# First image of a fused attention and cluster block: halves stored with 128 rows outermost, another order of its first stage, small weights loaded later

## The chip, the cores and the metric

The kernel runs on one core of a Trainium2 chip. The metric is the device time of one launch in microseconds (us); lower is better.

## The reference

The input x has 4 images of 256 channels and 64 x 64 pixels. Layer 0 is self-attention over the N = 4096 pixels of an image, with queries and keys of 32 channels:

```python
xf = x.reshape(B, C, N)
q = jnp.einsum('oc,bcn->bno', wq, xf) + bq
k = jnp.einsum('oc,bcn->bon', wk, xf) + bk[None, :, None]
attn = jax.nn.softmax(jnp.einsum('bnd,bdm->bnm', q, k), axis=-1)
v = jnp.einsum('oc,bcn->bon', wv, xf) + bv[None, :, None]
out = jnp.einsum('bcn,bmn->bcm', v, attn).reshape(B, Cc, H, W)
return gamma[0] * out + x
```

Layer 1 is a context-cluster block on the result: a group norm, features and values by 1x1 convolutions, an assignment of each pixel to one of four cluster centres per region and head, a projection added to x, then a second group norm with an MLP (1024 hidden channels, gelu), a scale and shift with relu, and a last 1x1 convolution with relu. All is float32. The change touches the start of layer 0 and the loading of weights.

## The kernel before, in words

An image is held in four SBUF tiles `xs[t]` of 128 partitions x 2 channel halves x 1024 pixels, each loaded by two DMAs of 512 KB (`load_x`). Blocks of NB = 512 pixels are the unit of queries and keys: NBLK = 8.

The order of the work is written out by hand (`tc.manual_schedule`): each engine, and SP as a queue of DMAs, runs its instructions in the order of the program. DMAs from SP and ACT share eight semaphores in turn, so a DMA can only be issued when the one eight places before it has landed. A DMA that waits holds back everything behind it on its engine, arithmetic included where the engine is ACT.

Attention of an image:

- **Projections and halves** (`halves_of`, L285 to L311). For four blocks at a time, PE makes queries or keys (`L295`): 4 row groups of 32 channels fill 128 partitions of a PSUM bank. ACT writes a rounded high half (`L304`), DVE the remainder as a low half (`L305`). Scores are then one product over 128 rows: queries stand as (high, high, low, low), keys as (high, low, high, low). That order is brought about through DRAM: four DMAs (`L311`) write the halves into a DRAM tile, and one DMA a block (`q_block` L355, `k_unit` L361) reads 128 rows of 512 back.
- `staged` (two projections into one PSUM tile with two banks) serves the first image twice ("first": keys and queries 0 to 3, "second": 4 to 7) and the queries of each later image, as `prepare`. `keys` makes the keys of later images, inside the cluster block of the image before.
- **Values** (`v_half`, `v_pair`): 16 pairs of value products (`L338`), each copied out of PSUM by ACT (`L346`). Two PSUM tiles are taken in turn.
- **Scores** (`score`, L375): unit u is one block of queries against one block of keys, 4 matmuls, copied out by ACT (L387, L388 or L397, L402), with running maxima on DVE (L392 or L399 to L404). `score(u)` first issues the read of keys u + 1. Two SBUF tiles hold keys.
- `fold`, `across`, `spread`: the maximum of a block over all keys, put on all partitions in PSUM (`mb`).
- **Weighting** (`weighting`): for 64 units, `exps` subtracts the maximum (DVE L480) and exponentiates (ACT L483), POOL sums (L485, L488), and PE accumulates values times weights (`weigh`, L493, 8 products of 512 columns a unit). Scores run ten units ahead. `prepare` of the next image is called at unit 61 of 64, after the fourth quarter of its `weigh`.

For the first image nothing comes before, so `alone` does it by itself: `staged("first")` with its half-writes issued by ACT, reads of keys 0 and queries 0 and 1, six value pairs, `staged("second")` with half-writes issued by SP, then eight scores with a value pair behind each, and two value pairs between the steps that make the maximum. For later images this lies inside the MLP of the image before.

At the very start the weights are loaded, in this order on SP: two loads of x tile 0, `wv_s`, `gbv`, x tiles 2 and 3, `pv_s`, `pc_s`, `h64`, `pool_w`, `mix` (two), `fvb`, `wproj_s` (two), `wpw_s`. ACT issues `wqk_s` (two), x tile 1 (two) and the query and key biases `bqk_s` (four). POOL turns two quarters of `wpw_s` (L147, L148) when they are there. `derived` (from L174), called at unit 1 of `weighting`, is the first reader of most of the small weights.

Of the kernel before, what the change touches and what calls it, by code (L numbers as in the profile page):

```python
# [46 lines left out]
def attention_then_cluster_block(  # L47
# [40 lines left out]
    def load_x(b, t, dma=nc.sync):  # L88
# [3 lines left out]
            dma.dma_start(out=xt[:, k, :], in_=xb[:, k, t * XT : (t + 1) * XT])  # L92
        return xt

    def loaded(name, ap, shape):
        t = const.tile(shape, F32, name=name)
        nc.sync.dma_start(out=t, in_=ap)
        return t

    xs0 = [load_x(0, 0)]
    wqk_s = const.tile([P, KC, 2, D], F32, name="wqk_s")
    for k in range(KC):
        nc.scalar.dma_start(out=wqk_s[:, k], in_=wqk[k * P : (k + 1) * P, :, :D])
    bqk_s = const.tile([P, 2], F32, name="bqk_s")
    xs0.append(load_x(0, 1, nc.scalar))
    for r in range(RG):
        nc.scalar.dma_start(
            out=bqk_s[r * D : (r + 1) * D, :], in_=pv[:D, PV["bq"] : PV["bq"] + 2]  # L110
        )
    wv_s = loaded("wv_s", wv.rearrange("(k p) m -> p k m", p=P), [P, KC, C])
    gbv = const.tile([P, KC], F32, name="gbv")
    nc.sync.dma_start(out=gbv, in_=bv.rearrange("(k p) -> p k", p=P))
    xs0 += [load_x(0, t) for t in range(2, N // XT)]
    pv_s = loaded("pv_s", pv, [P, NPV])
    pc_s = loaded("pc_s", pc.rearrange("(k p) n -> p k n", p=P), [P, KC, len(PC)])
# [1 line left out]

    pool_w = const.tile([P, 8, 32], F32, name="pool_w")  # L120
    nc.gpsimd.memset(pool_w, 0.0)
    nc.sync.dma_start(
        out=pool_w[:, :, :16], in_=consts[:, K_POOL : K_POOL + P].rearrange("p (j s) -> p j s", j=8)
    )

    own_w = {}
# [1 line left out]
    def load_mix(b):  # L128
        own_w["mix"] = swap.tile([P, KC, 2, 2 * ED + 32], F32, tag="mix", name=f"mix_{b}")
        for f in range(2):  # L130
            nc.sync.dma_start(
                out=own_w["mix"][:, :, f, 16 : 16 + 2 * ED],
                in_=wfv.rearrange("(k p) m -> p k m", p=P),
            )

    load_mix("first")
    fvb = const.tile([P, 2 * ED], F32, name="fvb")
    nc.sync.dma_start(out=fvb[:, ED:], in_=v_b.partition_broadcast(P))

    wproj_s = const.tile([ED + 1, C], F32, name="wproj_s")  # L140
    nc.sync.dma_start(out=wproj_s[:ED], in_=wproj)
    ipb = PC.index("proj_b")
    nc.sync.dma_start(out=wproj_s[ED:, :], in_=pc[:, ipb : ipb + 1].rearrange("c o -> o c"))

    wpw_s = loaded("wpw_s", wpw.rearrange("(k p) m -> p k m", p=P), [P, KC, C])
    pw_q = [wpw_s[:, k, h * P : (h + 1) * P] for k in range(KC) for h in range(2)]
    nc.gpsimd.tensor_tensor(pw_q[1], pw_q[1], pw_q[3], ALU.add)  # L147
    nc.gpsimd.tensor_scalar(pw_q[3], pw_q[3], -1.0, None, ALU.mult)  # L148

    ident = const.tile([P, P], F32, name="ident")  # L150
    make_identity(nc, ident)
# [80 lines left out]


    gab = const.tile([P, 2 * KC], F32, name="gab")
    probe = const.tile([P, 1], F32, name="probe")
    nc.gpsimd.memset(probe, 1.0)

    def table(f):

        nc.scalar.activation(probe, probe, f)  # L240
# [36 lines left out]
    def attention(b, xs):  # L277
# [4 lines left out]
        cells = small.tile([P, KC, NBLK, 4], F32, tag="cells", name=f"cells_{b}")  # L282
        qs, ks, slots, mxs, accs, tops, rdens, ts = {}, {}, {}, {}, {}, {}, {}, {}

        def halves_of(which, i, parts, ps, dma=nc.sync):  # L285

            col = 1 if which == "k" else 0  # L290
            if which not in own:
                own[which] = dram.tile([NBLK, 4, D, NB], F32, tag=which, name=f"{which}_{b}")
            for k in range(KC):
                for r in range(RG):
                    nc.tensor.matmul(  # L295
                        ps[r * D : (r + 1) * D],
                        wqk_s[:, k, col],
                        block(xs, k, 4 * i + r),
                        start=(k == 0),
                        stop=(k == KC - 1),  # L300
                    )
            bias = bqk_s[:, col : col + 1]
            hi, lo = parts
            nc.scalar.activation(hi, ps, AF.Identity, bias=bias)  # L304
            nc.vector.scalar_tensor_tensor(  # L305
                lo, ps, bias, hi.bitcast(F32), ALU.add, ALU.subtract
            )
            rows = own[which][4 * i : 4 * i + 4]
            for c in range(4):
                part = hi if c in ((0, 2) if which == "k" else (0, 1)) else lo  # L310
                dma.dma_start(out=rows[:, c], in_=part.bitcast(F32))  # L311

        def staged(name, which, dma=nc.sync):


            st = spool.tile([P, 4, NB], F32R, tag="s", name=f"st_{b}_{name}")
            ps = ps_s.tile([P, 2, NB], F32, tag="s", name=f"pr_{b}_{name}")
            for j, (w, i) in enumerate(which):
                halves_of(w, i, (st[:, 2 * j], st[:, 2 * j + 1]), ps[:, j], dma)

        def keys(i):

            ps = ps_m.tile([P, NB], F32, tag="m", name=f"kp_{b}_{i}")
            parts = [
                big.tile([P, NB], F32R, tag="k", bufs=2, name=f"hl{j}_{b}_{i}") for j in range(2)
            ]
            halves_of("k", i, parts, ps)

        vps = {}

# [17 lines left out]
        def v_pair(i):  # L348
            v_half(2 * i)
            v_half(2 * i + 1)  # L350

        def q_block(nb):

            qs[nb] = work.tile([P, NB], F32R, tag="q", name=f"q_{b}_{nb}")
            nc.sync.dma_start(out=qs[nb].bitcast(F32), in_=own["q"][nb].rearrange("c d n -> (c d) n"))  # L355

        def k_unit(u):

            g = u % GRP
            ks[u] = big.tile([P, NB], F32R, tag="k", bufs=2, name=f"k_{b}_{u}")  # L360
            nc.sync.dma_start(out=ks[u].bitcast(F32), in_=own["k"][g].rearrange("c d n -> (c d) n"))  # L361

        def score(u, hooks=None, later=None):

# [181 lines left out]

        def alone():

            staged("first", (("k", 0), ("q", 0)), nc.scalar)
            k_unit(0)  # L550
            q_block(0)
            q_block(1)
            for i in range(6):
                v_pair(i)
            for u in range(GRP):
                if u == 0:
                    staged("second", (("k", 1), ("q", 1)))
                hooks, maxima = [], []
                score(u, hooks, maxima)
                for f in hooks + maxima:  # L560
                    f()
                v_pair(u + 6)
            fold(0)
            half["dg"] = across(0)
            v_pair(GRP + 6)
            spread(0, half["dg"])
            v_pair(GRP + 7)
            exps(0)
            score(GRP)

# [25 lines left out]
        def weighting(ahead, fill, early, prepare):  # L596
# [3 lines left out]
            for u in range(units):  # L600
                nb, g = divmod(u, GRP)
                more = nb + 1 < NBLK
                if g == 0:
                    av = [
                        ps_a.tile([P, NB], F32, tag=f"a{c}", name=f"av{c}_{b}_{nb}")
                        for c in range(KC)
                    ]
                if g + 1 < GRP:
                    exps(u + 1)
                else:  # L610
                    gather(nb)
# [24 lines left out]
                weigh(u, av, 2)  # L636
                if g == GRP - 2 and more:
                    known(nb + 1, mb)
                due(u, 3)
                if g == GRP - 3 and more:  # L640
                    mb = highest(nb + 1)
                weigh(u, av, 3)
                if u == 1:
                    early()
                if u in biased:

                    t, c = biased[u]
                    nc.scalar.activation(
                        xs[t][:, c], xs[t][:, c], AF.Identity, bias=gbv[:, c : c + 1]
                    )  # L650
                if u == units - 3:
                    prepare()
                if g == 3 and nb + 2 < NBLK:
                    q_block(nb + 2)
                if g == GRP - 1 and more:
                    clear(nb, av)
# [1023 lines left out]
```

## Time and profile before

| | us |
|---|---|
| median of 3 runs (3314.1 to 3314.88) | 3314.72 |
| the profiled execution | 3316.3 |
| its span | 3314.5 |
| ACT busy in the span | 1679.6 |
| DVE busy | 2231.4 |
| POOL busy | 1929.9 |
| PE's weight loads (PEld, beside PE) | 1930.3 |

The span is that of the instructions in the profiled execution; the execution's own time is 1.8 us more. The mean granted TensorE clock is 0.991 of full speed. PE is TensorE's matmuls, ACT ScalarE, DVE VectorE, POOL GpSimd, SP SyncE; ACTq and SPq are DMA issues by those engines. A line of the timeline has start and length in us, engine, kernel line, operation, output and inputs, count, and in brackets how long the engine had stood idle and what released it.

From the timeline of the first 100 us, in order: the first projection starts at 5.21, the first high half at 13.59 (after the biases and a table load of 1.28), the first half-writes are issued at 14.31, the value products go on at 32.90, the second projections at 42.00, the first score at 47.37, the second at 69.78, the eighth at 87.88, and the first weighting product at 99.85. Each from the third to the eighth score, with its value pair, takes 2.65.

### The profile page before, as it was taken

What the parts mean: (1) busy time and instruction counts of PE and PEld (TensorE: products, weight loads), DVE (VectorE), ACT (ScalarE), POOL (GpSimd) and SP (SyncE); (2) the same over time, 40 slices, a digit from 0 to 9 for tenths busy, and PEclk for the clock granted to TensorE, in tenths of its full rate; (3) what the DMA queues carried; (4) which work ended last, traced back from release to release, by engine and by line L of the source; (5) the groups of instructions that cost most, each with busy time, mean ns of one, the idle gap of its engine ahead of it and who ended that gap; (6) DMA issues with size and microseconds to landing.
All of it is one profiled execution on the core that took longest, in us unless ns stands there. A gap on an engine that the chain in (4) does not pass through costs nothing.

```text
span 3314.5 us, 33083 instructions
## 1 busy us (share of the span) xinstructions
PE 3220.7 (97%) x11114; PEld 1930.3 (58%) x11114; DVE 2231.4 (67%) x3570; ACT 1679.6 (51%) x2253; POOL 1929.9 (58%) x1358
## 2 busy tenths in 40 slices
PE   4999999999999999999999999999999999999999
PEld 3544444778744444478864444447884444446786
DVE  1776775577777677466767777746776777765665
ACT  2655553445565555344556555535455555544444
POOL 0467567266457667636646667663654676673663
PEclk7999999999999999999999999999999999999999
DMA  4111112100111111210011111121011111110000
GB/s 143 51 51 42 48 48 91 45 26 29 36 58 48 48 45 42 102 40 26 29 42 51 48 39 54 41 105 36 20 39 54 41 53 48 39 52 1 13 20 26
DMA packets 87002, 154.78 MB, mean 47 GB/s; under 512 B 12496, under 2 KB 21296, under 8 KB 86832
## 3 DMA queue, kind: packets, MB, share of 16 engines
q1 hardware_dynamic: 84752, 149.45, 13.9%
q10 hardware_dynamic: 2080, 3.21, 0.3%
q8 instruction: 88, 1.44, 0.2%
q14 instruction: 82, 0.67, 0.1%
HBM read 118.96 MB, written 33.67 MB: 46 GB/s over the span
## 4 chain that ended last, share of the span: by engine, by line
PE 90%; DVE 5%; DMA 1%; ACT 1%; issue 1%; POOL 1%; SPq 0%; ACTq 0%; DVEq 0%; POOLq 0%
PE av L493 52%; PE mo L1309 9%; PE sc L375 7%; PE hq L1392 5%; PE hp L1392 3%; PE hr L1392 3%; PE fv L888 3%; PE vp L338 2%; PE mo L1293 1%; PE hq_pw L1392 1%; DVE st L993 1%; PE pw L1248 1%; PE hr_pw L1392 1%; PE hp_pw L1392 1%; DMA k<-k 1%
## 5 line engine op out<-in xcount | busy, mean ns | idle before, releaser
L493 PE MATMUL av<-s,v 128*128 128x512 f32 x4096 | 1796.3, 592 | 0.7 <-ACT s L483 0.7
L488 POOL TENSOR_TENSOR acc<-acc,s 128x1024 f32<-128x1024 f32 x448 | 1060.2, 2367 | 502.3 <-ACT s L483 481.8
L493 PEld LDWEIGHTS av<-s,v 128*128 128x128 f32 x4096 | 775.8, 190 | 896.1 <-issue 866.7
L483 ACT ACTIVATE s<-s 128x1024 f32<-128x1024 f32 x512 | 541.0, 1058 | 569.2 <-DVE s L480 549.0
L480 DVE TENSOR_TENSOR s<-s,mb 128x1024 f32<-128x1024 f32 x512 | 595.7, 1205 | 16.2 <-ACT mb L464 14.9
L401 DVE TENSOR_TENSOR top<-sc,top 128x1024 f32<-128x1024 f32 x196 | 239.1, 1220 | 291.1 <-PE sc L375 291.1
L1347 ACT ACTIVATE hs<-hs,pv_s 128x256 f32<-128x256 f32 x496 | 232.4, 502 | 343.1 <-DVE hs L1383 343.1
L375 PE MATMUL sc<-q,k 128*128 128x512 f32 x1024 | 371.1, 484 | 22.1 <-DMA k<-k 19.4
L1309 PE MATMUL mo<-hs,w 128*128 128x256 f32 x1512 | 385.2, 381 | 0.0
L1309 PEld LDWEIGHTS mo<-hs,w 128*128 128x128 f32 x1512 | 283.8, 190 | 46.3 <-ACT hs L1347 6.8
L404 DVE TENSOR_TENSOR top<-sc,top 128x1024 f32<-128x1024 f32 x196 | 240.0, 1225 | 81.5 <-ACT s L397 69.1
L375 PEld LDWEIGHTS sc<-q,k 128*128 128x128 f32 x1024 | 191.0, 189 | 160.9 <-issue 121.1
L397 ACT COPY s<-sc 128x1024 f32<-128x1024 f32 x224 | 224.6, 1003 | 116.1 <-PE sc L375 83.5
L402 ACT COPY s<-sc 128x1024 f32<-128x1024 f32 x224 | 227.6, 1016 | 109.8 <-DVE top L401 73.7
L1383 DVE TENSOR_TENSOR hs<-hq,hs 128x256 f32<-128x256 f32 x496 | 198.3, 420 | 79.6 <-PE hq L1392 69.6
L485 POOL TENSOR_TENSOR acc<-s 128x1024 f32<-128x1024 f32 x32 | 75.9, 2371 | 288.1 <-ACT s L483 288.0
L1316 POOL TENSOR_TENSOR hs<-hs 128x256 f32<-128x256 f32 x108 | 82.2, 761 | 184.3 <-ACT hs L1400 86.2
L338 PE MATMUL vp<-wv_s,x 128*128 128x256 f32 x512 | 133.1, 407 | 14.2 <-ACT v L346 14.2
L1383 DVE TENSOR_TENSOR hs<-hp,hs 128x256 f32<-128x256 f32 x124 | 52.1, 420 | 115.0 <-ACT hs L1400 115.0
L1392 PE MATMUL hr<-xn,w 128*128 128x256 f32 x496 | 127.8, 380 | 0.5 <-DVE hs L1383 0.5
L338 PEld LDWEIGHTS vp<-wv_s,x 128*128 128x128 f32 x512 | 99.5, 202 | 41.0 <-ACT v L346 16.4
L1392 PEld LDWEIGHTS hr<-xn,w 128*128 128x128 f32 x496 | 94.4, 191 | 18.0 <-issue 3.3
(271 smaller groups left out, 3501.5 us busy)
## 6 DMA issues: line engine op xcount, KB each, us to landing
k<-k SPq DMA_DIRECT2D x256, 256.0 KB
out<-xn SPq DMA_DIRECT2D x62, 256.0 KB
x<-in_x SPq DMA_DIRECT2D x30, 512.0 KB
q<-q SPq DMA_DIRECT2D x32, 256.0 KB
w<-in_w SPq DMA_DIRECT2D x8, 1024.0 KB
mr<-row_mx SPq DMA_DIRECT2D x28, 256.0 KB
rden<-row_rd SPq DMA_DIRECT2D x28, 256.0 KB
q<-st_queries SPq DMA_DIRECT2D x24, 256.0 KB
```

Of the source, the lines that this page charges most:

```text
L338: nc.tensor.matmul(vps[0][:, i % 2, :], xs[i * P // XT][:, k, o : o + P], wv_s[:, k, :], start=(k == 0), stop=(k == KC - 1),)
L375: nc.tensor.matmul(halves[r // 2][:, r % 2, :], k_s[:, r * P : (r + 1) * P], q_s, start=True, stop=True,)
L401: nc.vector.tensor_tensor(top, halves[1], top, ALU.max)
L404: nc.vector.tensor_tensor(top, halves[0], top, ALU.max)
L480: nc.vector.tensor_tensor(sh, sh, mxs[nb].unsqueeze(1).to_broadcast([P, 2, NB]), ALU.subtract)
L483: nc.scalar.activation(sh, sh, AF.Exp)
L488: nc.gpsimd.tensor_tensor(acc, acc, s[:, 2 * h : 2 * h + 2], ALU.add)
L493: nc.tensor.matmul(av[c], own["v"][:, RG * g + quarter, c * P : (c + 1) * P], slots[u][:, quarter, :], start=(g == 0 and quarter == 0), st ...
L1309: return nc.tensor.matmul(bank[:, half * HB : (half + 1) * HB], a[:, j], t, start=start, stop=stop)
L1347: nc.scalar.activation(src, src, AF.Gelu_apprx_tanh, bias=pvc("b1", P, j + 4 * (i > 1)))
L1383: nc.vector.tensor_tensor(dst, ps, term, ALU.add)
L1392: nc.tensor.matmul(out, w, x, start=True, stop=True)
```

## The change

1. **Layout in DRAM.** The DRAM tiles for halves were (block, 4 parts, 32 channels, 512 pixels); a half-write went to 4 blocks x 32 channels x 512. They become (4 blocks together, 128 rows, 4 parts, 512 pixels), so a half-write goes to 128 rows x 512. A block is read as its 32 rows x 4 parts; each still is one contiguous 256 KB. It holds for all images.
2. **Projections first.** `halves_of` is split: `projected` (PE alone) and `halves_of` (ACT, DVE and DMAs). `staged` makes both projections before any half.
3. **First image** (`alone`). The ACT table is loaded ahead; three value pairs come before `staged("first")`, whose half-writes are issued by SP; five pairs follow, then scores with pairs 8 to 15 behind them, so that none is left between the steps of the maximum.
4. **Loads.** `wv_s` is loaded ahead of x tile 1 in program order and stands third on SP as before; the four biases are issued by POOL. `gbv`, `pv_s`, `pc_s`, `h64`, `pool_w`, `wpw_s`, and `mix`, `fvb`, `wproj_s` are issued by SP after score 3 and its value pair (`load_rest`), with POOL's two operations on `wpw_s` behind them. On SP this is 11 DMAs after the read of keys 4 and before that of keys 5.
5. **Queries of later images**: `prepare` at unit 62 instead of 61.

The work of PE, ACT, DVE and POOL is the same in kind and number, but for the ACT table's one probe instruction.

```diff
+    probe = const.tile([P, 1], F32, name="probe")
+    nc.gpsimd.memset(probe, 1.0)
+    behind = []
     def loaded(name, ap, shape):
         t = const.tile(shape, F32, name=name)
-        nc.sync.dma_start(out=t, in_=ap)
+        behind.append(lambda: nc.sync.dma_start(out=t, in_=ap))
         return t
...
+    wv_s = const.tile([P, KC, C], F32, name="wv_s")
+    nc.sync.dma_start(out=wv_s, in_=wv.rearrange("(k p) m -> p k m", p=P))
     bqk_s = const.tile([P, 2], F32, name="bqk_s")
     xs0.append(load_x(0, 1, nc.scalar))
     for r in range(RG):
-        nc.scalar.dma_start(
+        nc.gpsimd.dma_start(
             out=bqk_s[r * D : (r + 1) * D, :], in_=pv[:D, PV["bq"] : PV["bq"] + 2]
         )
-    wv_s = loaded("wv_s", wv.rearrange("(k p) m -> p k m", p=P), [P, KC, C])
-    gbv = const.tile([P, KC], F32, name="gbv")
-    nc.sync.dma_start(out=gbv, in_=bv.rearrange("(k p) -> p k", p=P))
+    gbv = loaded("gbv", bv.rearrange("(k p) -> p k", p=P), [P, KC])
...
+    def load_rest():
+        load_mix("first")
+        nc.sync.dma_start(out=fvb[:, ED:], in_=v_b.partition_broadcast(P))
+        nc.sync.dma_start(out=wproj_s[:ED], in_=wproj)
+        nc.sync.dma_start(out=wproj_s[ED:, :], in_=pc[:, ipb : ipb + 1].rearrange("c o -> o c"))
+        for f in behind:
+            f()
+        nc.gpsimd.tensor_tensor(pw_q[1], pw_q[1], pw_q[3], ALU.add)
+        nc.gpsimd.tensor_scalar(pw_q[3], pw_q[3], -1.0, None, ALU.mult)
...
-        def halves_of(which, i, parts, ps, dma=nc.sync):
+        def projected(which, i, ps):
             col = 1 if which == "k" else 0
-            if which not in own:
-                own[which] = dram.tile([NBLK, 4, D, NB], F32, tag=which, name=f"{which}_{b}")
             for k in range(KC):
                 for r in range(RG):
                     nc.tensor.matmul(
...
+        def halves_of(which, i, hi, lo, ps, dma=nc.sync):
+            col = 1 if which == "k" else 0
+            if which not in own:
+                own[which] = dram.tile([NBLK // RG, P, 4, NB], F32, tag=which, name=f"{which}_{b}")
             bias = bqk_s[:, col : col + 1]
-            hi, lo = parts
             nc.scalar.activation(hi, ps, AF.Identity, bias=bias)
...
-            rows = own[which][4 * i : 4 * i + 4]
+            rows = own[which][i]
             for c in range(4):
                 part = hi if c in ((0, 2) if which == "k" else (0, 1)) else lo
                 dma.dma_start(out=rows[:, c], in_=part.bitcast(F32))
+        def stacked(which, nb):
+            i, r = divmod(nb, RG)
+            return own[which][i, r * D : (r + 1) * D].rearrange("d c n -> (d c) n")
...
             for j, (w, i) in enumerate(which):
-                halves_of(w, i, (st[:, 2 * j], st[:, 2 * j + 1]), ps[:, j], dma)
+                projected(w, i, ps[:, j])
+            for j, (w, i) in enumerate(which):
+                halves_of(w, i, st[:, 2 * j], st[:, 2 * j + 1], ps[:, j], dma)
...
         def alone():
-            staged("first", (("k", 0), ("q", 0)), nc.scalar)
+            table(AF.Identity)
+            for i in range(3):
+                v_pair(i)
+            staged("first", (("k", 0), ("q", 0)))
             k_unit(0)
             q_block(0)
             q_block(1)
-            for i in range(6):
+            for i in range(3, 8):
                 v_pair(i)
             for u in range(GRP):
                 if u == 0:
...
-                v_pair(u + 6)
+                v_pair(u + GRP)
+                if u == 3:
+                    load_rest()
             fold(0)
             half["dg"] = across(0)
-            v_pair(GRP + 6)
             spread(0, half["dg"])
-            v_pair(GRP + 7)
             exps(0)
             score(GRP)
...
-                if u == units - 3:
+                if u == units - 2:
                     prepare()
```

More of the change, by code (lines that the diff above doesn't have):

```diff
@@ L121, in attention_then_cluster_block @@
     nc.gpsimd.memset(pool_w, 0.0)
-    nc.sync.dma_start(
-        out=pool_w[:, :, :16], in_=consts[:, K_POOL : K_POOL + P].rearrange("p (j s) -> p j s", j=8)
+    behind.append(
+        lambda: nc.sync.dma_start(
+            out=pool_w[:, :, :16],
+            in_=consts[:, K_POOL : K_POOL + P].rearrange("p (j s) -> p j s", j=8),
+        )
     )
@@ L134, in load_mix @@
             )
-    load_mix("first")
     fvb = const.tile([P, 2 * ED], F32, name="fvb")
-    nc.sync.dma_start(out=fvb[:, ED:], in_=v_b.partition_broadcast(P))
     wproj_s = const.tile([ED + 1, C], F32, name="wproj_s")
-    nc.sync.dma_start(out=wproj_s[:ED], in_=wproj)
     ipb = PC.index("proj_b")
-    nc.sync.dma_start(out=wproj_s[ED:, :], in_=pc[:, ipb : ipb + 1].rearrange("c o -> o c"))
+    def load_rest():
[7 more added lines that the diff above has]
+        nc.gpsimd.tensor_scalar(pw_q[3], pw_q[3], -1.0, None, ALU.mult)
     wpw_s = loaded("wpw_s", wpw.rearrange("(k p) m -> p k m", p=P), [P, KC, C])
     pw_q = [wpw_s[:, k, h * P : (h + 1) * P] for k in range(KC) for h in range(2)]
-    nc.gpsimd.tensor_tensor(pw_q[1], pw_q[1], pw_q[3], ALU.add)
-    nc.gpsimd.tensor_scalar(pw_q[3], pw_q[3], -1.0, None, ALU.mult)
     ident = const.tile([P, P], F32, name="ident")
@@ L234, in attention_then_cluster_block @@
     gab = const.tile([P, 2 * KC], F32, name="gab")
-    probe = const.tile([P, 1], F32, name="probe")
-    nc.gpsimd.memset(probe, 1.0)
     def table(f):
@@ L326, in keys @@
             ]
-            halves_of("k", i, parts, ps)
+            projected("k", i, ps)
+            halves_of("k", i, *parts, ps)
         vps = {}
@@ L354, in q_block @@
             qs[nb] = work.tile([P, NB], F32R, tag="q", name=f"q_{b}_{nb}")
-            nc.sync.dma_start(out=qs[nb].bitcast(F32), in_=own["q"][nb].rearrange("c d n -> (c d) n"))
+            nc.sync.dma_start(out=qs[nb].bitcast(F32), in_=stacked("q", nb))
         def k_unit(u):
@@ L360, in k_unit @@
             ks[u] = big.tile([P, NB], F32R, tag="k", bufs=2, name=f"k_{b}_{u}")
-            nc.sync.dma_start(out=ks[u].bitcast(F32), in_=own["k"][g].rearrange("c d n -> (c d) n"))
+            nc.sync.dma_start(out=ks[u].bitcast(F32), in_=stacked("k", g))
         def score(u, hooks=None, later=None):
```

## The prediction

> **What bounds the kernel now.** I read part 1 of the page first, then busy time by stretch, then the timeline of the first 125 us with the chain of waits, and last every stretch in which PE stands still.
>
> ```profile
> PE 3220.7 (97%) x11114; PEld 1930.3 (58%) x11114; DVE 2231.4 (67%) x3570; ACT 1679.6 (51%) x2253; POOL 1929.9 (58%) x1358
> ```
>
> PE works 97% of the span: only its 94 us of idle time (3314.5 - 3220.7) and time at a reduced clock can be won. The stretches (PE busy, PEld, DVE, ACT, POOL, then PEclk, DMA share, GB/s) show where they lie:
>
> ```profile
> 5.20:20.70 15.50, 11.12 (x48) 4.07 (x48) 1.50 (x2) 2.66 (x3) 0.00 (x0) 1.00 0.80 250
> 20.70:32.90 12.20, 0.00 (x1) 0.00 (x1) 0.00 (x0) 0.64 (x2) 0.00 (x0) 0.61 0.52 162
> ...
> 51.50:69.80 18.30, 0.02 (x1) 0.06 (x1) 0.64 (x2) 0.59 (x1) 0.00 (x0) 0.57 0.33 122
> 69.80:90.60 20.80, 20.80 (x84) 17.41 (x84) 15.79 (x26) 16.35 (x20) 0.00 (x0) 0.89 0.28 77
> 90.60:99.90 9.30, 6.30 (x29) 4.40 (x27) 6.12 (x8) 2.90 (x6) 0.00 (x0) 1.00 0.08 28
> ...
> 585.00:605.00 20.00, 20.00 (x71) 11.30 (x72) 7.30 (x9) 6.03 (x8) 8.73 (x6) 1.00 0.26 100
> ```
>
> About 45 us of PE's idle time lie before 100 us, most of it in two holes of 12.2 and 18.3 us. In both, few of the DMA engines work. The timeline names the holders, and the chain says the same of the second hole:
>
> ```profile
> 32.26 1.07 ACT L346 COPY v<-vp 128x512 f32<-128x512 f32 x2 [13.38 <-DMA q<-st_first]
> 32.90 9.17 PE L338 MATMUL vp<-wv_s,x 128*128 128x256 f32 x32 [12.21 <-ACT v L346]
> ...
> 69.78 2.04 PE L375 MATMUL sc<-q,k 128*128 128x512 f32 x4 [18.28 <-DMA k<-k]
> 71.62 3.33 PE L338 MATMUL vp<-wv_s,x 128*128 128x256 f32 x8
> ...
> 583.00 1.92 PE L295 MATMUL pr_queries<-x,wqk_s 128*32 128x512 f32 x16 [1.65 <-DVE st_queries L305]
> ```
>
> ```profile
> 52.16 3.56 SPq L311
> 55.77 2.52 SPq L311
> 58.33 11.31 DMA k<-k
> ```
>
> First hole: ACT's queue also issues the eight writes of the first halves, each behind a DMA still in flight, so the copies of v that free PSUM come at 32.26. Second hole: SP issues eight more half-writes, then the read of keys 1, which lands at 69.6. At 583.00 PE waits 1.65 us for DVE between two projections; this recurs at 1394.67 and 2207.06 (images 1 to 3 being prepared).
>
> **What the skill says.** (1) "DMA: Bandwidth & Descriptors", section on why a DMA increments its semaphore by 16: a DMA runs on the largest k up to 16 that divides the slowest dimension of both patterns. The old DRAM side is 4x32x512, so k = 4; the new is 128x512, so 16. The trace agrees on the old: in 585 to 605, when only query half-writes run, the share is 0.26 at 100 GB/s, a quarter of the engines. (2) "TensorE: Matmul & The Clock Gate", Part 1: the array runs at half clock until some 3.4 us of activity. Agrees: PEclk 0.57 in the second hole; the two groups after it took 2.04 and 3.33 us where the same groups at 80 us take 1.28 and 1.89, a loss of 2.2. (3) The DMA page, "SWDGE vs HWDGE vs iDMA" and "Latency": DMAs from GpSimd have software-made descriptors, about 1 us to the first byte, some 2 us fixed. No DMA here is issued from POOL, so nothing shows it.
>
> **The change, part by part.** *Half-writes.* 262144 bytes at 100 GB/s are 2.6 us, eight 21 us. Sixteen engines at the same rate each (100/0.26 = 385 GB/s) give 0.68 us, eight 5.4 us: an estimate. The completion records support it: the output store, same rows on 16 engines, ends 2.1 us after issue. Reads are contiguous as before (2.6 us to landing).
>
> *The new order of the first image*, step by step:
> - PE starts with three value products and needs wv, complete at 8.9 in the records of before, behind the same two x loads: 8.9 against 5.2. This is a loss of 3.7 us.
> - Three products at 1.73 (a period of 80.80 to 83.45 is 2.65, of which scores take 0.92) are 5.2, plus 2.2 for the half clock: 16.3. Copies of v (0.58) keep up, ACT no longer issues half-writes and its table is loaded early (1.28 us, under the wait for x).
> - Keys and queries are projected together, 2 x 1.8: 19.9. The halves then follow as ACT 0.69, DVE 0.75, ACT 0.69, DVE 0.75 = 2.9, beside PE's next five products (8.7): 28.6; second projections 3.6: 32.2.
> - SP issues the first half-writes from 20.7 to 24.0; eight at 0.68 from 1.2 after the first issue end about 27.8. q block 0 is read after that, 2.8 us: 30.7. Score 0 wants it at 32.2: 1.5 us of cover. Its second PSUM half waits for DVE until 35.2 (0.93 and 1.59 us of such gaps were there before, 2.7 now). Product 8 ends at 37.5.
> - SP issues the second half-writes from 33.0; data 34.2 to 39.6; the read of keys 1 is behind all eight in SP's order and lands at about 40.4. PE waits 2.9. **Score 1: 40.4 instead of 69.8.**
> - Scores 1 to 7 are six periods of 2.65 (ACT 2.64, DVE 2.5 a period stay below): 15.9.
>
> *Small weights behind score 3.* The function issues 11 DMAs on SP after the read of keys 4 and before keys 5; their issues in the timeline sum to 5.2 us. Keys 4 goes out when score 2 is done, 44.1; so keys 5 at 49.6 rather than when score 3 is done (46.7), landing 52.3 to 53 behind wpw's 256 KB; score 5 wants it at 51.0. I charge 1.5; the lower end is 0, the upper 4.5, if a lane wait holds SP. The two POOL operations on wpw go ahead of POOL's first sum: free. What reads these weights (L174 at 113.9) comes 60 us after their issue.
>
> *Clock.* The PE gaps of 2.7 and 2.9 us may drop the clock: a 1.85 us gap did at 1484, one of 2.29 at 93 did not. One window of 3.4 us costs 1.7, two 3.4; I charge 1.5. Score 7 then starts at 40.4 + 15.9 + 1.5 + 1.5 = 59.3, against 87.88: 28.6 earlier.
>
> *Tail.* Products 14 and 15 leave it. They hid nothing there, as the DVE chain (maxima, fold, reduce, subtract) sets its length, and the copy of product 15 delayed the exponentials: 0.7 gained. PE is emptier there and may go cold: 0.5 charged (0 to 2), the rest under the 1.68 us gap at 124.16, which DVE and ACT set. Net 28.8.
>
> *Bias bqk from POOL.* Four DMAs, bounded by 0 and 4 x 3 = 12 us (page's figures, an estimate) after 0.9: at worst 13, needed at 19.9, so free with 7 us of cover. ident and the memsets queued behind on POOL are first needed at the fold.
>
> *Queries of later images.* Both projections before the halves remove 3 x 1.65 = 5.0. Moving them one unit later puts the last exponentials (DVE L480 at 586.38, behind the halves) ahead; after it PE has a unit of 16 products (6.9 us) as cover, and the sum on POOL (to 594.9) ends earlier. The half-writes on SP come 6 us later but end sooner; their reader is 60 us away. The faster key writes free SP only: no PE gap there waits on them.
>
> Sum: 28.8 + 5.0 = **33.8**. From the profiled span 3314.5 that is 3280.7 (its execution took 3316.3, 1.8 around the span); from the median 3314.72, 3280.9. I say **3281**.
>
> **Rivals.**
> - *Everything aligns:* no clock drop, keys 5 in time, and ACT allowed to split keys before the query projection ends: 1.5 + 1.5 + 1.8 = 4.8 more, 3276. For: the halves are separate banks. Against: before, the second projection waited for DVE on the first half, so the whole tile is tracked.
> - *More waits in its place:* keys 5 late by 4.5 (+3), two cold windows at score 1 and in the tail (+3.4), wv late by 1.5: gain 26, 3289. For: all sit on PE's path without cover.
> - *The query gaps aren't worth their length*, as the end of an image is a chain over DVE and POOL: 3286. Against: PE runs without a gap from 583 to 650.
> - *The layout doesn't spread the DMAs:* eight first writes end at 43, eight second at 64, score 1 at 65.5: gain 4.3 + 0.7 + 5.0 = 10, 3305. Against: the output store's 128 rows.
> - *Slower: bqk is late.* ACT waits in order for it before the first half; behind it stand the copies of v, so PE stops within two products. Each us after 19.9 costs one; from 19.9 + 33.8 = 54 us on the kernel is slower, at 60 it gives 3321. Only an unseen start-up cost of POOL's DMA path could do that.
>
> **How the numbers follow.** Forecast 52%, aligned 14%, more waits 15%, query gaps 11%, no spread 3% (2 of them inside the bound), late bqk 5% (1 inside the bound). Less than 0.2% (6.6 us) can't be told from no change here: faster 52 + 14 + 15 + 11 + 1 = 0.93; same 0.03; slower 0.04. Range 3273 to 3292: from the aligned case less some us of an earlier wv (0 to 3) to the upper ends of clock and keys 5. It leaves out no spread, late bqk and part of the tails.
>
> **What would show it.** Half-write stretches at a DMA share well over 0.26; no ACT copy of v waiting for a DMA; no hole of 12 or 18 us; score 1 near 40, keys 5 late by a few us behind the small weights, the first weighting product near 71; no 1.65 us gap in pr_queries. I am wrong if L316 waits for bqk, if keys 1 lands after 45, or if PE's gap reappears at the end of an image.

## The result and the profile after

The changed kernel takes 3290.24 us (median of 4 runs, 3289.91 to 3290.54) where the kernel before, on the same chip, takes 3314.8 (3314.1 to 3315.07): a ratio of 0.9926 [0.9909, 0.9943], 24.6 us less. Run again beside an experiment it gave 3288.4 against 3315.04, 0.9919 [0.9905, 0.9932]. The forecast was 3281 with a range of 3273 to 3292: the direction and most of the size hold, 9 us of the expected 33.8 did not come. Of these, 7.2 are in the profiled executions too (spans 3314.5 and 3287.9, so 26.6); the rest is that the profiled execution of before was 1.5 us above its median and that of after 0.3 below.

PE's line on the first part of the page of after:

```profile
PE 3220.5 (98%) x11114; PEld 1933.6 (59%) x11114; DVE 2232.6 (68%) x3570; ACT 1680.7 (51%) x2254; POOL 1933.1 (59%) x1362
```

PE is as busy as before (3220.7), in a span 26.6 us shorter. So it is idle time that went, 94 us down to 67. Busy time by stretch shows from where (after; start and end, length, then busy PE, PEld, DVE, ACT, POOL, then PEclk, which is the granted share of the TensorE clock, DMA share, GB/s):

```profile
8.79:20.60 11.81, 11.81 (x57) 7.45 (x57) 0.00 (x0) 1.76 (x3) 0.00 (x0) 1.00 0.47 191
20.60:32.96 12.36, 12.36 (x73) 8.39 (x73) 1.50 (x2) 4.20 (x7) 0.00 (x0) 1.00 0.67 234
32.96:42.32 9.36, 3.12 (x15) 2.11 (x13) 2.80 (x4) 3.88 (x5) 0.00 (x0) 0.97 0.82 278
42.32:57.89 15.57, 12.17 (x48) 9.99 (x49) 9.99 (x16) 9.77 (x12) 0.91 (x2) 0.91 0.54 128
57.89:64.77 6.88, 6.88 (x24) 5.60 (x25) 3.23 (x6) 4.19 (x5) 0.09 (x1) 0.75 0.20 53
64.77:76.56 11.79, 7.21 (x24) 4.33 (x22) 8.70 (x12) 4.22 (x6) 0.00 (x0) 0.86 0.11 38
...
571.00:574.00 3.00, 3.00 (x8) 1.10 (x6) 0.29 (x1) 0.00 (x0) 0.00 (x0) 1.00 1.06 380
```

The two holes of 12.2 and 18.3 us are gone: from 8.79 to 32.96 PE has no idle time at all, and the first half-writes lie under its work (second row). The last row, where only query half-writes run, has a DMA share of 1.06 at 380 GB/s; the like stretch before had 0.26 at 100. The third and fourth rows hold what is left of the two holes, 6.2 and 3.4 us, and the timeline of after names it:

```profile
8.79 8.21 PE L358 MATMUL vp<-wv_s,x 128*128 128x256 f32 x24 [8.79 <-DMA wv_s<-in_wv]
...
20.66 0.69 ACT L316 ACTIVATE st_first<-pr_first,bqk_s 128x512 fp32r<-128x512 f32 x1 [3.04 <-PE pr_first L299]
21.38 2.10 SPq L323 DMA_DIRECT2D k<-st_first  x4
...
36.16 0.70 PE L395 MATMUL sc<-q,k 128*128 128x512 f32 x2 [2.50 <-DVE st_second L317]
...
38.34 9.48 SPq L381 DMA_DIRECT2D k<-k  x4
...
42.32 2.05 PE L395 MATMUL sc<-q,k 128*128 128x512 f32 x4 [3.73 <-DMA k<-k]
...
47.88 0.94 SPq L139 DMA_DIRECT2D mix_first<-in_wfv  x2
...
51.50 1.27 PE L395 MATMUL sc<-q,k 128*128 128x512 f32 x4
...
52.13 0.47 SPq L103 DMA_DIRECT2D h<-in_consts  x1
...
53.42 0.37 SPq L128 DMA_DIRECT2D pool_w<-in_consts  x1
...
54.52 21.70 SPq L381 DMA_DIRECT2D k<-k  x6
...
57.89 1.27 PE L395 MATMUL sc<-q,k 128*128 128x512 f32 x4 [3.40 <-DMA k<-k]
58.96 3.51 PE L358 MATMUL vp<-wv_s,x 128*128 128x256 f32 x8
...
76.56 1.98 PE L513 MATMUL av<-s,v 128*128 128x512 f32 x4 [0.69 <-ACT s L503]
...
563.42 3.64 PE L299 MATMUL pr_queries<-x,wqk_s 128*32 128x512 f32 x32
```

ACT's first half waits for the projection and not for the biases, so these were in time. Score 1 starts at 42.32 instead of 69.78, after 3.73 us of waiting for keys 1; score 5 waits 3.40 for keys 5; the group after score 5 runs cold, that is at half clock (3.51 us instead of 1.89). The first weighting product comes at 76.56 instead of 99.85, 23.3 earlier. The 32 query products of image 1 stand in one line without a wait, and those of images 2 and 3 have none either. The chain of waits of after passes through exactly these two reads of keys and the half-writes' issue ahead of the first (start, length, what held the end):

```profile
36.39 0.55 SPq L323
...
37.66 0.63 SPq L323
...
38.34 3.84 DMA k<-k
...
54.52 3.24 DMA k<-k
```

The account of the profiled pair closes: 23.3 to the first weighting product, 5.0 in the queries, less some 1.4 because after 110 us the clock record has 30.8 us of the span at half clock instead of 28.0 (an estimate, half of the difference). That is 26.9, and 26.6 was measured.

### The profile page after: what moved, and what is told of

Its sections match the earlier page's. It is cut to its first block, busy times and chain, and to the rows that moved or that the text cites. A ratio compares the mean times of both kernels' runs of the same rounds, so it can differ in the third digit from the quotient of the medians.

```text
span 3287.9 us, 33084 instructions
## 1 busy us (share of the span) xinstructions
PE 3220.5 (98%) x11114; PEld 1933.6 (59%) x11114; DVE 2232.6 (68%) x3570; ACT 1680.7 (51%) x2254; POOL 1933.1 (59%) x1362
## 4 chain that ended last, share of the span: by engine, by line
PE 93%; DVE 4%; ACT 1%; issue 1%; POOL 1%; DMA 0%; SPq 0%; ACTq 0%; DVEq 0%; POOLq 0%
PE av L513 52%; PE mo L1332 10%; PE sc L395 7%; PE hq L1415 5%; PE hp L1415 3%; PE hr L1415 3%; PE fv L911 3%; PE vp L358 3%; PE mo L1316 1%; PE hq_pw L1415 1%; PE pw L1271 1%; PE hr_pw L1415 1%; PE hp_pw L1415 1%; PE op L1023 1%; DVE hs L1406 0%
```

## The experiments

Each median (us) stands beside that of the kernel before on the same chip; the gain is their difference. The ratio, with its 95% interval, is taken over all runs, so it can differ a little from that of the medians.

| run | median (range) | before | ratio [95%] | gain |
|---|---|---|---|---|
| the change | 3290.24 (3289.91–3290.54) | 3314.8 | 0.9926 [0.9909, 0.9943] | 24.6 |
| the change, again | 3288.4 (3284.27–3291.19) | 3315.04 | 0.9919 [0.9905, 0.9932] | 26.6 |
| layout alone | 3289.0 (3287.86–3289.75) | 3315.5 | 0.9921 [0.9906, 0.9936] | 26.5 |
| all but the layout | 3318.05 (3313.91–3320.53) | 3315.5 | 1.0007 [0.9999, 1.0016] | −2.6 |
| small weights behind score 7 | 3285.14 (3282.16–3286.71) | 3315.5 | 0.9907 [0.9891, 0.9924] | 30.4 |
| keys 1 ahead of the writes | 3283.67 (3281.24–3285.5) | 3315.5 | 0.9905 [0.989, 0.9919] | 31.8 |
| both of these | 3279.82 (3277.97–3281.39) | 3317.14 | 0.9889 [0.9875, 0.9904] | 37.3 |
| both, two pairs back in the tail | 3282.17 (3274.85–3282.52) | 3317.14 | 0.9891 [0.9877, 0.9906] | 35.0 |
| projections before all values | 3292.38 (3290.49–3293.09) | 3317.14 | 0.9927 [0.9912, 0.9941] | 24.8 |
| halves between, all images | 3294.01 (3290.75–3295.3) | 3317.14 | 0.9934 [0.9917, 0.995] | 23.1 |
| halves between, later queries only | 3294.53 (3293.63–3296.08) | 3315.04 | 0.9937 [0.9924, 0.9949] | 20.5 |
| queries at unit 61 | 3287.5 (3284.73–3288.37) | 3316.2 | 0.9916 [0.99, 0.9933] | 28.7 |
| old order, layout, keys 1 ahead | 3284.82 (3283.78–3286.16) | 3316.2 | 0.9908 [0.9893, 0.9922] | 31.4 |

**Layout alone.** The kernel before, with only its DRAM tiles laid out anew (the reads of a block follow the new layout; not shown here):

```diff
-own[which] = dram.tile([NBLK, 4, D, NB], ...)
+own[which] = dram.tile([NBLK // RG, P, 4, NB], ...)
...
-rows = own[which][4 * i : 4 * i + 4]
+rows = own[which][i]
```

> The kernel before with only the DRAM layout changed. Theory (the layout carries most of what the first image gained, because half-writes on 4 DMA engines filled both holes): the copies of v no longer wait for queued half-writes, keys 1 lands near 42 instead of 69.6, the first weighting product starts near 73 instead of 99.9; the three 1.65 us gaps between query projections stay. 3291 us, 3286 to 3297. Rival (the new order and the later loads carry it): over 3304.

It gains 26.5 us, as much as the whole change. It is the writes that are faster: the read of a block of keys that runs alone takes as long with either layout, from issue to landing 2.58 us at 75.92 before and 2.66 at 59.20 after. The timeline, ACT's and PE's lines:

```profile
14.08 3.21 ACTq L311 DMA_DIRECT2D k<-st_first  x4
...
19.92 3.33 ACTq L311 DMA_DIRECT2D q<-st_first  x4
23.29 1.07 ACT L350 COPY v<-vp 128x512 f32<-128x512 f32 x2 [4.67 <-DMA q<-st_first]
...
23.93 7.17 PE L342 MATMUL vp<-wv_s,x 128*128 128x256 f32 x32 [1.82 <-ACT v L350]
...
43.06 2.04 PE L379 MATMUL sc<-q,k 128*128 128x512 f32 x4 [2.53 <-DMA k<-k]
...
73.93 3.70 PE L497 MATMUL av<-s,v 128*128 128x512 f32 x8 [0.70 <-ACT s L487]
```

ACT still issues the first half-writes itself, but they hold its copy of v for 4.67 us instead of 13.38, so the first hole shrinks from 12.21 to 1.82 us; and score 1 starts at 43.06 after 2.53 us of waiting instead of 18.28. The first weighting product comes at 73.93. That is 2.6 us earlier than in the profile of the whole change, but four profiles of the change's own first image lie between 72.37 and 78.53 (see the clock, below). So no gain of the other edits shows in the first image, and whether they cost anything there isn't shown.

**All but the layout.** The changed kernel with the tiles of before (the edit above, backwards).

> The changed kernel with the old DRAM layout: order, loads and projections first stay. Theory (layout): eight half-writes again take 21 us each time, score 1 comes near 66, and what is left of the gain are the three query gaps (5 us) and a little of the first image: 3309 us, 3305 to 3313. Rival (order and loads carry the gain): under 3300.

It came out above even the theory's range, and can't be told from the kernel before. PE's and SP's lines of its timeline:

```profile
20.90 3.21 SPq L323 DMA_DIRECT2D k<-st_first  x4
...
48.20 2.05 PE L394 MATMUL sc<-q,k 128*128 128x512 f32 x4 [15.70 <-DMA q<-q]
48.88 11.42 SPq L323 DMA_DIRECT2D q<-st_second  x4
...
71.81 2.04 PE L394 MATMUL sc<-q,k 128*128 128x512 f32 x4 [18.15 <-DMA k<-k]
...
88.35 2.04 PE L394 MATMUL sc<-q,k 128*128 128x512 f32 x4 [2.85 <-DMA k<-k]
...
106.96 5.29 PE L512 MATMUL av<-s,v 128*128 128x512 f32 x6 [0.70 <-ACT s L502]
```

The first hole isn't filled, it moves: value products ahead of the projections start the slow writes at 20.90 instead of 14.31, so score 0 waits 15.70 us for its queries. The second hole stands at 18.15, and a wait of 2.85 before score 5 is new. The first weighting product comes 7.1 us later than before (106.96 instead of 99.85), and the queries of later images give 5.0 back. So only fast writes make the new order harmless; it doesn't replace them.

**Small weights behind score 7.** The changed kernel, with one line of another value:

```diff
-                if u == 3:
+                if u == GRP - 1:
                     load_rest()
```

> The changed kernel with the small weights issued behind score 7 instead of score 3, where SP has no key read to send for some 10 us. Theory (the 11 issues hold keys 5 back by 3.4 us and the clock drop behind that wait costs 1.5): 3285.3 us, 3284 to 3287, no wait before score 5. Rival (the wait only moves to keys 9, or the weights are late for their readers): 3289 or more.

As expected. SP's lines and, below, PE's:

```profile
51.96 8.26 SPq L381 DMA_DIRECT2D k<-k  x4
60.27 0.94 SPq L139 DMA_DIRECT2D mix_first<-in_wfv  x2
...
53.31 1.27 PE L395 MATMUL sc<-q,k 128*128 128x512 f32 x4
54.42 1.89 PE L358 MATMUL vp<-wv_s,x 128*128 128x256 f32 x8
55.95 1.27 PE L395 MATMUL sc<-q,k 128*128 128x512 f32 x4
```

The small loads go out behind the keys, score 5 (55.95) follows score 4 (53.31) by one period (2.64 here), and the wait doesn't reappear elsewhere. The place behind the fourth score costs 4 to 6 us, by the medians beside the two runs of the change.

**Keys 1 ahead of the writes.** In the changed kernel, SP reads keys 1 ahead of the second half-writes instead of behind them. It belongs to the first four blocks and doesn't depend on them.

```diff
                 if u == 0:
+                    k_unit(1)
                     staged("second", ...)
...
-            if u + 1 < units:
+            if u + 1 < units and u + 1 not in ks:
```

> The changed kernel with the read of keys 1 issued ahead of the second half-writes, of which it needs none. Theory (the 3.7 us wait before score 1 is SP's order, 8 x 0.67 us of writes ahead of the read, and the clock drop behind it costs 1.2): 3285.5 us, 3284.5 to 3288. Rival (the wait moves to keys 2, which still stands behind the writes): 3289 to 3291.

A little better than expected. The timeline of PE:

```profile
36.06 0.70 PE L395 MATMUL sc<-q,k 128*128 128x512 f32 x2 [2.32 <-DVE st_second L317]
42.15 1.17 PE L395 MATMUL sc<-q,k 128*128 128x512 f32 x4 [1.01 <-DMA k<-k]
53.28 1.17 PE L395 MATMUL sc<-q,k 128*128 128x512 f32 x4 [2.93 <-DMA k<-k]
```

Score 1 starts at 38.14 without a wait. Score 2 now waits 1.01 for keys 2, which stay behind the writes. Of 3.73 us, 2.7 went for good: score 2 starts at 42.15 instead of 46.20. The wait before score 5 stays, as it must. In the profiled execution the clock also stayed at full speed from 14.22 to 65.42, through three waits. How much of the gain is this, and whether it is luck or the edit, these runs don't show (see the last section).

**Both.** The two edits above in one kernel.

> Both edits: small weights behind score 7 and keys 1 read ahead of the second half-writes. Theory (two waits in a row on PE's path, both real): the savings add, 5.1 + 6.5 with the clock drops counted once, 3279.5 us, 3277.5 to 3281.5. Rival (the one hides the other): 3283.

The savings add. Its timeline, SP's lines and two of PE's:

```profile
30.61 0.43 SPq L381 DMA_DIRECT2D k<-k  x1
...
37.91 16.35 SPq L381 DMA_DIRECT2D k<-k  x7
54.31 0.94 SPq L139 DMA_DIRECT2D mix_first<-in_wfv  x2
...
60.58 1.02 PE L435 MATMUL tt<-ident,top 128*128 128x128 f32 x4 [2.29 <-DVE top L429]
...
67.64 3.70 PE L513 MATMUL av<-s,v 128*128 128x512 f32 x8 [0.70 <-ACT s L503]
```

From score 1 at 38.71 to score 7 at 55.29 PE has no wait above 0.4 us. The next wait is the tail's 2.29 for DVE; the first weighting product comes at 67.64. With 37.3 us this is the best kernel of the study, some 11 to 13 us better than the change itself.

**Both, two pairs back in the tail.** From that kernel, three value pairs instead of five before the second projections, and the last two again between the steps of the maximum.

```diff
-            for i in range(3, 8):
+            for i in range(3, 6):
...
-                v_pair(u + GRP)
+                v_pair(u + 6)
...
+            v_pair(GRP + 6)
             spread(0, half["dg"])
+            v_pair(GRP + 7)
             exps(0)
```

> As the kernel with both edits, but with value pairs 14 and 15 back between the steps of the maximum, as before the change, and three pairs instead of five before the second projections. Theory (in the tail PE idles and its clock drops, so two pairs there are free, while before the second projections they are on PE's path): score 2 comes some 2.5 us sooner, 3277 us, 3275 to 3279. Rival (the forecast's view that the tail's pairs only delay the exponentials): 3280 or more.

The rival holds: no gain. PE's lines:

```profile
32.14 1.17 PE L395 MATMUL sc<-q,k 128*128 128x512 f32 x4 [3.15 <-DVE st_second L317]
...
41.10 2.05 PE L395 MATMUL sc<-q,k 128*128 128x512 f32 x4 [3.41 <-DMA k<-k]
```

The second projections start at 25.35, 3.5 earlier, but score 0 then waits 3.15. The profile names DVE, which ended at 32.04, and the queries landed at 32.01: either alone would have held it as long. Score 2 waits 3.41 for keys 2. So what was taken out ahead of the second projections had covered the writes and reads. The tail is longer too, as the rival's view has it: 13.63 us from score 7 to the first weighting product, instead of 12.35. One of four runs took 3274.85, so the median's 2.4 us over the kernel above is not a difference that these runs can show.

**Projections before all values.** In the changed kernel the three value pairs ahead of the first projections go behind them.

```diff
-            for i in range(3):
-                v_pair(i)
             staged("first", (("k", 0), ("q", 0)))
-            for i in range(3, 8):
+            for i in range(8):
```

> The changed kernel with its first projections at the front again and all eight first value products behind them. Theory (PE has the same work up to the second projections, and x tile 1, complete only near 12.4 us, holds the projections as wv holds the products): within 1.5 us of the changed kernel, 3290 us. Rival (three products first are worth the wait for x): 3293 or more.

No difference (0.9927). PE starts at 5.01 but waits 2.65 and 0.54 us for x, and reaches the second projections at 29.92 instead of 29.33. The 3.7 us that the prediction charged for the late start are real, and in this pair of profiles they are paid back: 3.2 are the waits for x, which the three products of the change fill.

**Halves between the projections**, first for all images (in `staged`, `halves_of` again directly behind each `projected`), later for the queries of images 1 to 3 alone:

```diff
                 projected(w, i, ps[:, j])
-            for j, (w, i) in enumerate(which):
+                if name == "queries":
+                    halves_of(...)
+            for j, (w, i) in enumerate(which if name != "queries" else ()):
                 halves_of(...)
```

> The changed kernel with each half made right behind its projection, as before. Theory: the 1.65 us wait of PE for DVE comes back at images 1 to 3 (5.0 us) and once in the first image (1.7), where the second stage breaks even, since its halves are also done sooner: 3296.5 us, 3294.5 to 3298. Rival (the waits are absorbed at the end of an image): 3290 to 3292.

> The changed kernel with the halves between the two projections again for the queries of images 1 to 3 alone; the first image keeps both projections ahead. Theory (the query gaps are worth their whole length, since nothing else on the way takes their place): the three gaps of 1.65 us come back in pr_queries and the time is 5.0 us over that of the unchanged order measured beside it, 3.5 to 6.5 with its scatter. Rival (the first run with halves between, only about 2.6 us over, had the right size: the chain over DVE and POOL at the end of an image absorbs part of a gap): 0 to 2.5 us over.

> The changed kernel once more, five rounds beside the one with halves between for later queries, as its base: 3289 to 3292 with a ratio near 0.9926 by both theories. It also shows how much of a run's profile repeats: keys 5 should again stand 3 to 3.7 us late, with score 1 at 42 to 43; whether the clock falls to half after these two gaps may differ.

For all images it came out just under the theory. In its profile the first image is ready earlier than in the profile of the change (first weighting product at 74.77 instead of 76.56), so it couldn't price the queries. The second run can: 3294.53 beside 3288.4, 6.1 us more on one chip, inside 3.5 to 6.5, and no run of the one lies among those of the other. The rival's 0 to 2.5 falls. From its view of the tile pr_queries (who waited for it: us, times) and its timeline:

```profile
PE pr_queries L299: 5.0, 3
```

```profile
568.96 1.92 PE L299 MATMUL pr_queries<-x,wqk_s 128*32 128x512 f32 x16 [1.65 <-DVE st_queries L317]
```

The 5.0 us come back as three waits of 1.65, and the time shows no sign that the end of an image absorbs them. The 6.1 is not exact: in the first image, where the two kernels are the same, their profiles already lie 2.7 us apart. The change itself, run again, took 3288.4, just under the 3289 to 3292 expected. Score 1 came at 41.94 (42 to 43 expected) after a wait of 2.40; score 5, after a wait of 2.85, came 3.20 us later than one period behind score 4, inside the 3 to 3.7.

**Queries at unit 61.** `prepare` back to its old place.

```diff
-                if u == units - 2:
+                if u == units - 3:
```

> The changed kernel with the queries of later images prepared at unit 61 again, projections still first. Theory (the 5 us come from the projections being first; moving them a unit later is free either way, the last exponentials having a unit of 6.9 us as cover): no wait in pr_queries, within 1 us of the changed kernel, 3290 us. Rival (the move is what removes the wait, or the late exponentials of unit 63 hold PE): 3292 or more.

The rival falls: no wait in pr_queries, and the time isn't above that of the change. Its 3287.5 lies a little below the theory's 1 us around 3290, but inside the runs of the change repeated. The move is worth nothing that these runs can tell.

**Old order, layout, keys 1 ahead.** The kernel before with the new layout, both projections first, unit 62 and the edit for keys 1: so the old order of values, ACT as issuer, early small weights.

> The kernel before with the new layout, projections first, queries at unit 62 and keys 1 read ahead; its first order (projections, then six pairs, pairs in the tail), loads and biases on ACT stay. Theory (with the layout, the new order and the later loads of the first image are worth nothing; only projections first and keys 1 ahead still are): 3281.5 us, 3279 to 3284.5. Rival (value products first and deferred loads gain with the layout): 3286 or more.

Between the two: just above the theory's 3284.5, under the rival's 3286. Timeline, ACT and PE:

```profile
17.99 6.40 ACTq L311 DMA_DIRECT2D q<-st_first  x4
...
24.43 1.07 ACT L353 COPY v<-vp 128x512 f32<-128x512 f32 x2 [6.47 <-DMA q<-st_first]
25.07 9.56 PE L345 MATMUL vp<-wv_s,x 128*128 128x256 f32 x32 [7.12 <-ACT v L353]
```

Here even fast writes hold ACT for 6.40 us, and PE waits 7.12 behind the copy of v. ACT's DMAs share the eight slots with SP, whose small loads lie between them; that these cause it is read from the order of the slots, and was not tried. The first weighting product comes at 74.53, where the kernel with both edits has 67.64. So the rest of the first stage (the new order, SP as the issuer of the first half-writes, the biases on POOL and the late small weights) is worth some 6 us together (31.4 to 37.3 by the medians, from two chips), once keys 1 and keys 5 don't wait behind something else. Which of them is worth how much within these 6 us was not separated.

## Why the prediction was right, and where it was too large

**Half-writes on 16 engines: right, and nearly the whole gain.** The completion records of the eight query writes of image 1 end 0.70 us apart (570.24 to 575.17), where before they end 2.56 apart (588.35 to 606.29); 0.68 was estimated. The rule that the forecast took from the Trainium skill ("DMA: Bandwidth & Descriptors", why a DMA increments its semaphore by 16) is confirmed on both sides: each of the old writes, with 4 as the slowest dimension on the DRAM side, shows 4 completions as its data lands, 4.5 us and more behind a first one right after its issue; each of the new ones shows 16. Beside other loads the writes are slower: 0.91 us apart for the first image's first eight, which ended at 30.11 instead of 27.8 (the forecast's own terms, 20.7 + 1.2 + 8 x 0.68, give 27.3). So queries 0 landed at 32.82, only 0.14 ahead of score 0, where 1.5 was forecast: that this was not one more wait is luck. The rival without a spread is out (its price was wrong too: a gain of 10, where the change with the old layout lost 2.6), and so is that of late biases: their four DMAs were complete at 9.24 and needed at 20.66. What the forecast did not ask is how much the layout gives alone: as much as all parts together (26.5).

**Score 1 at 40.4: it was 42.32.** The forecast let eight writes end at 39.6, with 0.68 each; they ended at 41.77. They started 0.75 us later (at 33.75), the first ended at 36.12, and the other seven took 0.81 each. So of the 2.2 us, 1.2 come from the start and the first write and 0.9 from the other seven. The order itself (keys 1 behind all eight) was foreseen and priced as a wait of 2.9. What was not asked is whether it had to be: the experiment with keys 1 ahead gains 5 to 7 us.

**Small weights: 1.5 charged, 3.7 paid.** This is the step that failed most. The forecast summed 5.2 us of issues and let keys 5 go out at 49.6. On the chip the first small load was issued at 47.88 and keys 5 at 54.52, 6.6 us on. The issues took 5.4 us, the steps between them 0.4, and SP stopped for 0.82: the issue of h64 (`h` in the view) ends at 52.60, and pool_w's begins at 53.42, because the slot it wants was used eight places earlier by the second half of mix, which landed at 53.35. Such a wait for a slot (the forecast's "lane wait") had been named as the upper bound (4.5) and was set aside for the middle. The read of keys 5 itself then took 3.24 us. The late load moved score 5 from one period behind score 4 to 6.39 us behind it, 3.74 more. Undone alone, it gives 4 to 6 us back.

**Clock: 1.5 charged, 2.8 paid** up to score 7. Scores 1 to 2 took 3.88 us and scores 5 to 7 6.88, where 2.65 and 5.30 are the periods: 1.23 + 1.58. A window at half clock fell on the end of the one wait and began 0.9 us behind the other, where the forecast had allowed for one in two. But this size is one draw. Three of the experiments run the first image with the same program as the change, and over the same scores their profiles lost anything from nothing to 5.0 us:

| profile | score 1 at | score 5 late by | lost to the clock | first weighting product |
|---|---|---|---|---|
| the change | 42.32 | 3.74 | 2.8 | 76.56 |
| the change, again | 41.94 | 3.20 | 2.8 | 75.85 |
| queries at unit 61 | 41.76 | 2.95 | none | 72.37 |
| halves between, later queries only | 42.11 | 3.91 | 5.0 | 78.53 |

Score 5 is late against one period of 2.65 behind score 4; the clock's loss is what scores 1 to 4 and 5 to 7 took beyond 2.65 each. The late keys are in all four, so they are what the forecast had wrong; that the clock's charge came out 1.3 too small is chance.

**The tail: right in sum.** From score 7 to the first weighting product 11.77 were forecast, and 11.79 measured (11.97 before). The 0.86 of PEclk in that stretch shows the cold window that was charged.

The three terms keys 1, small weights and clock are the whole miss of the first image in the profile of the change: 1.9 + 2.2 + 1.3 = 5.4 of 5.5 us (76.56 instead of 71.07). The forecast's rival of "more waits in its place", at 3289, named the second and the third, and comes nearest to what happened; its third part, a late wv, did not come (complete at 8.65, and 8.9 was forecast), and it didn't name a later score 1. The forecast took a third of one bound and not half of the other, as if they were independent. In this profile they aren't: both half-clock windows came with the two waits for keys, so a wait that comes late costs its length and may cost a half-clock window as well.

**Queries: 5.0 forecast, right.** This is shown by putting the halves back for them alone (6.1 by the medians, 5.0 by the waits). The forecast gave the gain to both projections being ahead, not to unit 62, and that holds.

## What to carry to other kernels

Price a DMA by how many engines its outermost dimension lets it use, before moving anything to hide it: a new layout of the DRAM tiles did here what the whole hand-made reordering could not do without it. When loads are deferred on an in-order queue, look at what the queue must issue next and when PE wants it; eleven small loads were 6.0 to 6.6 us of queue time in the four profiles above, and they belong behind the last transfer with a consumer nearby. Where one wait has a bound of several us and sits on an uncovered path, add to its price a range for the clock behind it: here nothing to 5.0 us for two such waits.

## What was not expected of the hardware

**The clock falls on a grid of 3.41 us, and its phase isn't the kernel's.** In the clock records every stretch at half speed, but for the one that the end of the span cuts off, is a multiple of 3.41 us long, and in the profile of the change the three in the first image start at 41.75, 58.82 and 72.47, five and four such steps apart. The Trainium skill ("TensorE: Matmul & The Clock Gate", Part 1, what's actually happening) describes such a free-running window of 3413 ns; the records agree. The section on HAM oscillation (HAM is its name for the monitor that gates the clock) gives a rule, no idle gap of PE over some 3.4 us. Keeping under it was not enough here: in the change run again a wait of 2.45 was followed by a half-clock step at 36.35. With keys 1 ahead, waits of 2.32, 1.01 and 2.93 were followed by none before 65.42. So a wait of 2 to 3 us has a chance, not a price. Runs of one kernel lie up to 7.7 us apart (3274.85 to 3282.52 with two pairs back in the tail); how much of that is the clock isn't shown. The phase alone does not settle what a wait costs: the change run again and the queries at unit 61 have nearly the same one (their first half-clock steps start at 36.35 and 36.45), and lost 2.8 us and nothing. Starting the kernel at a chosen phase wasn't tried.

**Later half-clock time differs between kernels that do the same there.** Between 110 us and the end of the span it sums to 30.8 us in the profile of the change, 24.3 in that of its repetition and 21.0 with the layout alone. If each us costs PE half a us, some 5 us of a comparison of two single profiles may be this (an estimate). Between the layout alone and the whole change it is more than the luck of one profile: the mean granted clock is 0.995 or 0.996 in all four runs of the layout alone, and 0.992 to 0.994 in all nine of the change. On average they are 0.0023 apart, which is at most some 7 us of 3288 (an estimate). That can make up for the 5 us of the queries that the layout alone lacks, and so the two come out equal. Why the change is granted less of the clock isn't shown.

**Small loads land late in company.** In the change, the second half of mix landed 5.0 us after its issue and fvb behind it after 4.7, while the first half-write of each of the first image's two groups of eight landed after 2.4. The late landing of mix, not the issues, cost SP its 0.82 us at pool_w.
